# A graph and feed-forward kernel on one core: count chunks and checks moved ahead of the attention terms, and four PSUM banks for turned blocks

## The chip, the cores and the metric

The kernel runs on one core of a Trainium2 chip. The metric is the device time of one execution in microseconds (us), as the median of repeated runs. One more execution was taken with the hardware profiler; all views below are of that one.

## The reference

The program applies four layers to 3125 nodes of 256 features each, with a residual around every layer: a graph attention network, a mixture of experts shared by all nodes, a graph convolution network and a routed mixture of experts. The change is at the very beginning of the first layer, whose first part is:

```python
h = (x @ W).reshape(N, H, C)                      # 4 heads of 256
al_s = jnp.einsum('nhc,hc->nh', h, a_src)
al_d = jnp.einsum('nhc,hc->nh', h, a_dst)
e = jax.nn.leaky_relu(al_s[src] + al_d[dst], NEG_SLOPE)
m = jax.ops.segment_max(e, dst, num_segments=N)
ex = jnp.exp(e - m[dst])
denom = jax.ops.segment_sum(ex, dst, num_segments=N)
alpha = ex / denom[dst]
out = jax.ops.segment_sum(h[src] * alpha[:, :, None], dst, num_segments=N)
```

There are 100,000 edges, sorted by destination. `x` is layer-normalized before it enters. The same edges serve the second attention and the convolutions, so the kernel counts them once into a matrix.

## The kernel before, in words

Nodes are padded to 25 blocks of 128 rows. Edges are worked in 391 chunks of 256 (two tiles of 128). The class that the change touches runs two things at once in one long loop. The first is counting: for each chunk VectorE (and partly ScalarE) makes one-hot rows of the edges' keys, TensorE multiplies them into a PSUM bank, ScalarE copies most columns of the result into an accumulator in SBUF and VectorE adds the shared first column. `count_step(i)` (line 1738 on) is a software pipeline of that: it makes chunk i (lines 1669, 1672, for later chunks also 1675 and 1678 on ScalarE), multiplies chunk i-1 (1686), adds chunk i-3 (1708) and keeps chunk i-2 (1703). Hot rows have three buffers, the PSUM results three banks. Chunks below 20 take both one-hot parts from VectorE; of later ones two in three take the second part from ScalarE.

The second is the sum over edges for the attention: `edge_step` gathers the source rows with their attention terms by an indirect DMA on GpSimd (1797), weighs them, spreads the weights and multiplies (1863, 1869), and adds into sums per destination (1880). One edge step covers one chunk of the edges that do not belong to the first two blocks of destinations; those two blocks are done densely (2045), once the first piece of counts is finished.

Ahead of the loop lies a stage called `before` (the function `run`). In it x is loaded and normalized block by block and the edges' keys are made (`keys`, 1508 to 1525). The projections of x onto the attention vectors are needed for every node: `u1` holds W1 times the attention vectors (1573), each of the 25 blocks of x is turned by TensorE (2138), copied by ScalarE out of PSUM (2142), and multiplied by `u1` into one PSUM bank `pl` (2146). The turned blocks are also stored to DRAM in groups of five (2144). VectorE then copies `pl` to `sd` (2151), and `first_terms` reduces maxima (1587 to 1590), takes them over the partitions on GpSimd (1592), and makes the terms (1599 to 1614); the source terms go into the gathered table (1601), the destination terms and the weights of the nodes' loops into tables of their own (1605, 1615). Between its two halves six count steps run.

Two more things are in that stage: `edge_starts` with `check` (1465 to 1493), which work out on one partition where each chunk's edges begin and whether the shortcuts hold, and `attention_vectors("2", ...)`, which prepares W2's vectors for the second attention (line 1573 again, from W2 loaded at 2125).

After the stage, `open_sums` takes banks and buffers for the edge sums and clears two banks (1764), the first 24 tiles of rows are gathered, `new_sums(0)` begins the first sums with the loops of the first nodes (1912 to 1939, which wait for the loads 1921 and 1923), with one count step for each of its five tasks, and two more count steps follow. Then the loop runs one count step in each iteration. The edge steps are spread over it: 45 over the iterations from `i0` to `d1`, a fixed count, and the rest by the chunk's number.

What sets the order: on VectorE the stage `before` keeps the order in which it is written (`k.in_order` over that engine). On the other engines a scheduler places instructions when the program is built, by their dependences and the pools' buffers. Instructions of `open_sums` that need nothing from the stage may also be placed inside it. In the loop, TensorE, VectorE and ScalarE keep the written order. SyncE (SP) issues most DMAs, in one order of its own.

Of the kernel before, what the change touches and what calls it, by code (L numbers as in the profile page):

```python
# [19 lines left out]
PSUM = bass.MemoryType.PSUM  # L20
# [1373 lines left out]
class FirstLayer:  # L1394
# [698 lines left out]
    def run(self, src_cols, dst_cols, dst_rows, x_in, keep, stats, u2):  # L2093

        tc, nc, k, I = self.tc, self.nc, self.k, self.I
        with ExitStack() as ctx:
            pool = ctx.enter_context(tc.tile_pool(name="edges", bufs=1, reuse_waits="tile"))
            self.open_counts(ctx, pool)
            w1 = pool.tile([P, 2, 4 * D], F32, name="w1_all")
            with tc.tile_pool(name="before", bufs=1, reuse_waits="tile") as tmp, \  # L2100
                    tc.tile_pool(name="ps_in", bufs=1, space=PSUM, reuse_waits="tile") as psum, \
                    tc.tile_pool(name="ps_turn", bufs=2, space=PSUM, reuse_waits="tile") as turn:
                start = len(nc.cur_bb.bb.instructions)
                self.bounds(dst_rows, tmp)
                self.load_edges(src_cols, dst_cols, tmp)
                nc.gpsimd.dma_start(w1, I["L0_gnn_W1"].rearrange("(c p) f -> p c f", p=P))
                for b in range(0, NB, GB):
                    last_x = nc.sync.dma_start(
                        k.x[:, b:b + GB, :],
                        x_in[b * P:(b + GB) * P, :].rearrange("(b p) f -> p b f", p=P))  # L2110
                nc.vector.memset(k.rows[:, :, D:], 1.0)
                groups = [self.norm_rows(
                    k.x[:, b:b + GB, :],
                    self.table[b * P:(b + GB) * P, :D].rearrange("(b p) f -> p b f", p=P), tmp)
                    for b in range(0, NB, GB)]
                u1 = tmp.tile([P, 2, 8], F32, name="u1")
                for g in range(GR + 1):
                    if g < GR:
                        next(groups[g])
                    if g > 0:  # L2120
                        next(groups[g - 1])
                self.count_starts(tmp)
                self.attention_vectors("1", tmp, u1, w1.rearrange("p c (k f) -> p k c f", k=4))
                w2 = tmp.tile([P, 8, D], F32, name="w2")
                load = nc.gpsimd.dma_start(w2, I["L0_gnn_W2"].rearrange("(c p) f -> p c f", p=P))
                tc.add_manual_dep(load.ins, self.placed.ins.name, ORDER)
                tc.add_manual_dep(load.ins, last_x.ins.name, SYNC)
                self.keys(tmp)
                pl = psum.tile([P, 512], F32, name="pl")
                sd = tmp.tile([P, NB, 8], F32, name="sd")  # L2130
                i = 0
                for b in range(NB):
                    if b % 4 == 0:
                        self.count_step(i)
                        i += 1
                    pt = turn.tile([P, 512], F32, name="turn")
                    for c in range(2):
                        nc.tensor.transpose(pt[:, ts(c, P)], k.x[:, b, ts(c, P)], k.ident)
                    if b % GB == 0:
                        xt5 = tmp.tile([P, 2, GW], F32, name="xt", bufs=GR)  # L2140
                    xt = xt5[:, :, ts(b % GB, P)]
                    nc.scalar.copy(xt, pt[:, :2 * P].rearrange("p (c n) -> p c n", c=2))
                    if b % GB == GB - 1:
                        nc.sync.dma_start(self.turned[:, :, (b + 1) * P - GW:(b + 1) * P], xt5)
                    for c in range(2):
                        nc.tensor.matmul(pl[:, 8 * b:8 * b + 8], lhsT=xt[:, c, :],
                                         rhs=u1[:, c, :], start=(c == 0), stop=(c == 1))
                self.edge_starts(tmp)
                self.check(tmp)
                self.attention_vectors("2", tmp, u2, w2.rearrange("p (k c) f -> p k c f", c=2))  # L2150
                nc.vector.tensor_copy(sd.rearrange("p b k -> p (b k)"), pl[:, :8 * NB])
                parts = self.first_terms(sd, pool)
                next(parts)
                for _ in range(6):
                    self.count_step(i)
                    i += 1
                next(parts)
                k.in_order({}, start, [mybir.EngineType.DVE])
            self.open_sums(ctx, w1, stats)
            for c in range(RB * BC):  # L2160
                self.fetch(c)
            for task in self.new_sums(0):
                task()
                self.count_step(i)
                i += 1
            self.tasks.extend(self.new_sums(1))
            for m in range(2):
                for c in range(self.size[m]):
                    self.window(m, c)
            self.count_step(i)  # L2170
            i += 1
            self.place_edges(0)
            self.pick_terms(0)
            self.count_step(i)
            i += 1
            self.place_edges(1)
            self.weigh_edges(0)
            self.spread_edges(0)
            self.open_dense()
            e = s = 0  # L2180
            i0, d0 = i, CUT[1] + 6
            engines, last = [mybir.EngineType.PE, mybir.EngineType.DVE, mybir.EngineType.Activation], {}
            start = len(nc.cur_bb.bb.instructions)

            d1 = d0 + 3
            while i < C1 + 3 or e <= NE or s < len(self.steps) or self.tasks or self.later:
                if i < C1 + 3:
                    self.count_step(i)
                self.counted = i >= C1 + 3
                if i == d0:  # L2190
                    self.lead(0)
                later, self.later = self.later, []
                if self.tasks:
                    self.tasks.popleft()()
                share = (FIRST * (i - i0) / (d1 - i0) if i < d1 else
                         FIRST + (NE + 1 - FIRST) * (i - d1) / (C1 - d1))
                while e <= NE and e <= share:
                    self.edge_step(e)
                    if e == NE:
                        last_piece = self.through_w1(AS - 1)  # L2200
                        self.tasks.extendleft(reversed(last_piece[:-8]))
                        self.tasks.extend(last_piece[-8:])
                    e += 1
                while s < len(self.steps) and i > d0 + 3 and \
                        s * (C1 - 12 - d0) <= (i - d0 - 3) * len(self.steps):
                    self.dense_step(s)
                    s += 1
                for f in later:
                    f()
                start = k.in_order(last, start, engines)  # L2210
                i += 1
# [490 lines left out]
```

## Time and profile before

| | |
|---|---|
| median of 3 runs | 2530.82 us (2530.34 to 2532.02) |
| the profiled execution's own time | 2636.26 us |
| its span | 2634.5 us |
| mean granted TensorE clock in it | 0.931 |
| busy: TensorE, VectorE, ScalarE, GpSimd | 86%, 52%, 44%, 32% |

The profiled execution is 105 us longer than the median, so a sum made from its durations stands against 2636.26 first.

The stretches at the start, from the view of busy time by windows (us busy of each engine, granted clock, share of the DMA engines):

| stretch, us | PE | DVE | ACT | POOL | clock | DMA |
|---|---|---|---|---|---|---|
| 42.8 to 52.4 | 9.59 | 9.39 | 0.00 | 0.00 | 1.00 | 0.49 |
| 52.2 to 68.5 | 16.30 | 0.32 | 4.84 | 0.00 | 1.00 | 0.22 |
| 68.3 to 84.4 | 3.16 | 15.33 | 1.71 | 0.00 | 1.00 | 0.11 |
| 84.4 to 98 | 4.94 | 12.78 | 4.91 | 2.13 | 1.00 | 0.32 |
| 98 to 131 | 7.13 | 13.22 | 3.23 | 23.79 | 1.00 | 1.03 |

How to read the profile: a row of the timeline gives the start and the duration in us, the engine, the line in the kernel's source, the operation with its output and inputs, and how many were merged (x). What stands in brackets is how long the engine stood idle before, and which instruction, of which engine, released it. PE is TensorE, PEld its weight loads, DVE VectorE, ACT ScalarE, POOL GpSimd, SP SyncE; SPq rows are DMA issues. A transfer's own duration isn't in these rows.

### The profile page before, as it was taken

Reading aid. Unit: us, or ns where it says so; the run is one execution under the profiler, and the core shown is the slowest. Engines: PE = TensorE matmul, PEld = TensorE weight load, DVE = VectorE, ACT = ScalarE, POOL = GpSimd, SP = SyncE. Lnnn points to the kernel's source line nnn. Section 1 sums busy time; section 2 is a strip of 40 time slices with the busy share of each in tenths; the row PEclk is TensorE's granted clock in tenths of the full one; section 3 lists DMA queues with packets and bytes.
Section 4 is the critical chain, followed back from the end, with each engine's and each line's share of the span. In section 5 each row is a group of like instructions: output and inputs, shape, how many; then the busy total and the mean of one; then the engine's idle time right before and its main releaser. Section 6 shows DMA issues by size and latency. Waiting matters only on the chain. (4 is left out here: it accounts for less than half of the span.)

```text
span 2634.5 us, 38636 instructions
## 1 busy us (share of the span) xinstructions
PE 2263.8 (86%) x11821; PEld 1827.0 (69%) x11821; DVE 1376.1 (52%) x4332; ACT 1153.5 (44%) x2553; POOL 833.4 (32%) x805
## 2 busy tenths in 40 slices
PE   4277789888888888598999989979999998999997
PEld 4155566666666665387888768868877666888886
DVE  6666657466776786514888833433335654111110
ACT  3167655545555554342444434543433434222221
POOL 1465566666676775010000030000001122212221
PEclk9977988888989998899999989989999988999998
DMA  6633446464656665499221110004324426666662
GB/s 219 88 103 89 128 108 183 114 179 119 173 158 175 190 175 149 131 378 304 81 75 63 50 36 0 1 31 145 114 100 139 140 100 195 168 186 180 175 193 54
DMA packets 241723, 354.97 MB, mean 135 GB/s; under 512 B 45360, under 2 KB 182931, under 8 KB 237794
## 3 DMA queue, kind: packets, MB, share of 16 engines
q1 hardware_dynamic: 197762, 253.10, 30.6%
q0 software_dynamic: 40176, 94.81, 14.2%
q10 hardware_dynamic: 3568, 4.47, 0.7%
q8 instruction: 99, 1.62, 0.3%
q14 instruction: 118, 0.97, 0.1%
HBM read 266.60 MB, written 86.86 MB: 134 GB/s over the span
## 5 line engine op out<-in xcount | busy, mean ns | idle before, releaser
L1797 POOL DMA_INDIRECT edge_rows<-table,pick x566 | 608.7, 1075 | 320.2 <-PE edge_sums L1863 107.6
L1863 PE MATMUL edge_sums<-edge_moves,edge_rows 128*128 128x120 f32 x2264 | 351.6, 305 | 37.1 <-DVE agg L1880 30.6
L1863 PEld LDWEIGHTS edge_sums<-edge_moves,edge_rows 128*128 128x128 f32 x2264 | 327.2, 217 | 74.3 <-DVE agg L1880 41.6
L1092 PE MATMUL po<-parts,cnt_r 128*128 128x512 f32 x1250 | 328.2, 416 | 9.4 <-ACT cnt_r L1086 9.4
L1686 PE MATMUL ps<-hot_key,hot_lo 128*128 128x350 f16 (+2 forms) x782 | 205.3, 356 | 106.1 <-DVE acc L1708 49.2
L1703 ACT CAST acc<-ps 128x325 f32 (+2 forms) x391 | 178.1, 455 | 255.5 <-DVE acc L1708 111.9
L1092 PEld LDWEIGHTS po<-parts,cnt_r 128*128 128x128 f32 x1250 | 239.4, 197 | 70.6 <-ACT cnt_r L1086 10.2
L854 PE MATMUL po<-h,w 128*128 128x257 f32 x1250 | 277.5, 382 | 6.7 <-DVE w L845 4.4
L854 PEld LDWEIGHTS po<-h,w 128*128 128x128 f32 x1250 | 236.5, 191 | 43.1 <-DVE w L845 6.4
L1669 DVE TENSOR_SCALAR hot_key<-iota_key,key 128x350 f16<-128x350 f16 (+2 forms) x782 | 231.5, 324 | 34.1 <-PE ps L1686 25.6
L2578 ACT ACTIVATE hid<-ph,ffn_b 128x256 f32<-128x256 f32 x232 | 109.9, 474 | 298.2 <-PE ph L2576 298.2
L2576 PE MATMUL ph<-xe,ffn_w 128*128 128x256 f32 x928 | 210.1, 382 | 2.0 <-DVE xe L2555 2.0
L2586 PE MATMUL py<-ffn_w,hid 128*128 128x256 f32 x928 | 209.5, 384 | 0.0
L2590 POOL DMA_INDIRECT out<-y,to x58 | 90.4, 1558 | 350.1 <-DVE y L2589 269.1
L2576 PEld LDWEIGHTS ph<-xe,ffn_w 128*128 128x128 f32 x928 | 173.9, 191 | 28.9 <-DVE xe L2555 2.2
L2586 PEld LDWEIGHTS py<-ffn_w,hid 128*128 128x128 f32 x928 | 176.5, 193 | 23.4
L1686 PEld LDWEIGHTS <-hot_lo 128*128 128x128 f16 x782 | 62.4, 104 | 160.0 <-issue 60.4
L839 ACT ACTIVATE z<-z,att_cols 128x640 f32<-128x640 f32 x125 | 103.1, 828 | 153.0 <-DVE z L837 130.1
L1675 ACT ACTIVATE hot_lo<-iota_key,lo 128x128 f16<-128x128 f16 x494 | 169.0, 391 | 0.0
L1880 DVE TENSOR_TENSOR agg<-agg,edge_sums 128x126 f32 (+1 forms) x283 | 87.0, 307 | 145.4 <-PE edge_sums L1869 43.9
L1086 ACT CAST cnt_r<-cnt_h 128x1920 fp32r<-128x1920 f16 x50 | 89.9, 1799 | 133.4 <-PE po L1092 130.4
L2045 PE MATMUL po<-x_rows,w 128*128 128x257 f32 x400 | 129.5, 451 | 3.6 <-issue 3.6
(403 smaller groups left out, 3368.2 us busy)
## 6 DMA issues: line engine op xcount, KB each, us to landing
ffn_w<-in_L_ffn_W SPq DMA_DIRECT2D x58, 1024.0 KB
cnt_h<-cnt SPq DMA_DIRECT2D x50, 800.0 KB
rows<-blank SPq DMA_DIRECT2D x109, 258.0 KB
cnt<-acc SPq DMA_DIRECT2D x50, 400.0 KB
cnt<-cnt SPq DMA_DIRECT2D x25, 800.0 KB
normed<-first_out SPq DMA_DIRECT2D x20, 640.0 KB
first_out<-first SPq DMA_DIRECT2D x56, 192.0 KB
edge_rows<-table,pick POOLq DMA_INDIRECT x566
```

Source lines behind the costliest of these rows:

```text
L854: nc.tensor.matmul(pos[i][:, :D + 1], lhsT=w[:, ts(i, P)], rhs=moving[:, j, :D + 1], start=(j == 0), stop=(j == NB - 1))
L1092: nc.tensor.matmul(pos[b], lhsT=c[:, j - j0, ts(b, P)], rhs=parts[i][:, j].rearrange("p a m -> p (a m)"), start=(j == 0), stop=(j == NB - 1))
L1669: nc.vector.tensor_scalar(h[:, u, :NB * w], self.wide[:, :NB * w], self.key[:, t:t + 1], None, op0=ALU.is_equal)
L1675: nc.scalar.activation(l[:, u, :], self.wide[:, :P], AF.Abs, bias=self.lo[:, t:t + 1], scale=-1.0)
L1686: self.nc.tensor.matmul(ps[:, :n], lhsT=l[:, u, :], rhs=h[:, u, :n], start=(u == 0), stop=(u == CT - 1))
L1703: self.nc.scalar.copy(self.acc[g][:, :, ds(o + 1, width(c) - 1)], self.parts[c][:, :, 1:])
L1797: self.nc.gpsimd.indirect_dma_start(out=self.ring[:, e % (RB * BT), :], out_offset=None, in_=self.table, in_offset=bass.IndirectOffsetOnAx ...
L1863: nc.tensor.matmul(ps[:, f * 4 * w:f * 4 * w + EW], lhsT=self.rows_of(m)[:, e, ts(f, P)], rhs=self.spread[m % 2][:, e * 4 * w:e * 4 * w + EW],
L2045: self.nc.tensor.matmul(self.pos[i][:, :D + 1], lhsT=w[:, ts(i, P)], rhs=self.k.rows[:, j, :], start=(j == 0), stop=(j == NB - 1))
L2576: nc.tensor.matmul(ph, lhsT=w1[:, c, ts(f, P)], rhs=xe[:, c, :], start=(c == 0), stop=(c == 1))
L2578: nc.scalar.activation(hid[:, f, :], ph, AF.Gelu, bias=b1[:, f:f + 1])
L2586: nc.tensor.matmul(py, lhsT=hid[:, f, ts(i, P)], rhs=w2[:, f, :], start=(f == 0), stop=(f == NF - 1))
```

## The change

In the stage before the loop, the seven count steps that stood in the loop over the 25 blocks (one at every fourth block) become two, ahead of that loop. The edges' starts, the checks and W2's vectors, which stood behind the loop over blocks, come ahead of it, behind these two count steps. The six count steps between the halves of the terms stay where they are, and all later count steps follow on with the next chunk's number, so that the loop begins with chunk 15 instead of chunk 20. The pool of PSUM banks for turned blocks gets four banks instead of two. Lines behind the block loop have numbers lower by one after the change; those inside it are higher by two.

```diff
-                    tc.tile_pool(name="ps_turn", bufs=2, space=PSUM, reuse_waits="tile") as turn:
+                    tc.tile_pool(name="ps_turn", bufs=4, space=PSUM, reuse_waits="tile") as turn:
...
                 self.keys(tmp)
+                for i in range(2):
+                    self.count_step(i)
+                i = 2
+                self.edge_starts(tmp)
+                self.check(tmp)
+                self.attention_vectors("2", tmp, u2, w2.rearrange("p (k c) f -> p k c f", c=2))
                 pl = psum.tile([P, 512], F32, name="pl")
                 sd = tmp.tile([P, NB, 8], F32, name="sd")
-                i = 0
                 for b in range(NB):
-                    if b % 4 == 0:
-                        self.count_step(i)
-                        i += 1
                     pt = turn.tile([P, 512], F32, name="turn")
...
                         nc.tensor.matmul(pl[:, 8 * b:8 * b + 8], lhsT=xt[:, c, :],
                                          rhs=u1[:, c, :], start=(c == 0), stop=(c == 1))
-                self.edge_starts(tmp)
-                self.check(tmp)
-                self.attention_vectors("2", tmp, u2, w2.rearrange("p (k c) f -> p k c f", c=2))
                 nc.vector.tensor_copy(sd.rearrange("p b k -> p (b k)"), pl[:, :8 * NB])
```

## The prediction, made before the changed kernel ran

> **What bounds the kernel now.** The whole page comes first: 2634.5 us of span, PE 86% busy, DVE 52%. Its chain of waits names a stretch of the last DMA only, so it says nothing about the start. The change lies in the first 130 us, so I went to the timelines of that stretch, engine by engine. VectorE:
>
> ```profile
> 45.28 0.75 DVE L1515 TENSOR_TENSOR rel<-dst,key 128x566 f32<-128x566 int32 x1
> ...
> 50.37 0.27 DVE L1669 TENSOR_SCALAR hot_key<-iota_key,key 128x200 f16<-128x200 f16 x1
> ...
> 68.87 0.27 DVE L1669 TENSOR_SCALAR hot_key<-iota_key,key 128x200 f16<-128x200 f16 x1 [16.34 <-PE ps L1686]
> ...
> 72.05 0.29 DVE L1465 TENSOR_SCALAR begin<-ends_all 1x283 f32<-1x283 f32 x1
> ...
> 78.86 0.40 DVE L1573 SCALAR_TENSOR_TENSOR att_scr<-w,att 128x256 f32<-128x256 f32 x1
> ...
> 84.39 0.35 DVE L2151 COPY sd<-pl 128x200 f32<-128x200 f32 x1
> ```
>
> VectorE has made three chunks by 52.5 us, then stands 16.34 us until TensorE has multiplied chunk 0 (there are three buffers of hot rows). Behind this wait are queued four more chunks, the starts and checks (L1465 on), W2's vectors (L1573) and the copy of the attention sums (L2151). TensorE shows why it is late:
>
> ```profile
> 38.83 2.27 PE L2138 MATMUL turn<-ident,x_rows 128*128 128x128 f32 x8 [1.91 <-ACT xt L2142]
> 42.81 9.56 PE L2146 MATMUL pl<-u,xt 128*128 128x8 f32 x44 [1.71 <-DVE att_scr L1573]
> 52.23 0.67 PE L2138 MATMUL turn<-ident,x_rows 128*128 128x128 f32 x2
> ...
> 66.77 1.71 PE L2146 MATMUL pl<-u,xt 128*128 128x8 f32 x8
> 68.33 1.16 PE L1686 MATMUL ps<-hot_key,hot_lo 128*128 128x200 f16 x6
> ```
>
> With two banks twelve of 25 blocks are turned before the small products begin; thirteen follow, alternating with products. The chunks come behind all of it, at 68.3. SyncE's and GpSimd's timelines say who waits for 84.4:
>
> ```profile
> 92.72 0.37 SPq L1601 DMA_DIRECT2D table<-s_terms  x1
> ```
> ```profile
> 97.96 1.23 POOL L1797 DMA_INDIRECT edge_rows<-table,pick  x1 [2.96 <-PE ps L1686]
> ```
>
> The rows' terms are stored after the copy, and the first gather starts 5.2 us after that issue. So the copy at 84.39 sets the gathers, and they the loop.
>
> [...] checks that need nothing from chunk 0 ran only after the 16.34 us. [...] Three for counts, one for sums and two for turned blocks make 6; with four, 8. No bank is free then for the two edge sums that are cleared early (L1764). In the kernel before these memsets ran at 7.22 and 8.56 us, unwaited. [...] between 94 and 131 us engines are nearly always busy at 133 GB/s, with 9,645 of 12,457 packets under 512 B.
>
> **Part by part.** VectorE's order in the changed program is written out by its build: 2 chunks, starts, checks, vectors, copy, 6 chunks. I use the trace's durations.
>
> Removed ahead of the copy: 50.37 to 72.05 is 21.68 us for seven chunks with the stall. Two chunks take 50.37 to 51.75, 1.38. That is 20.30 saved, as long as no other wait takes its place.
>
> Unchanged work behind: starts and checks 72.05 to 78.86, 6.81; vectors 78.86 to 84.39, 5.53.
>
> Four banks: TensorE's order becomes nearly all transposes, then the products. Four blocks took 2.27 us, 0.57 each. With four banks two more blocks are turned before 38.83, so block 22 ends near 38.8 + 13 x 0.57 = 46.2, and block 24 near 47.4. With no lead it would be 1.1 later. Fifty products at 9.56/44 = 0.217 take 10.9: done at 58 to 60. The copy comes at about 66, so 6 to 8 us of VectorE's work covers this end; were that gone, the products would set it.
>
> New wait: L1764's first memset now stands right ahead of L1515 (45.28) and waits for ScalarE's copy of block 22. That copy took 0.37: 46.6 to 47.7, a stall of 1.3 to 2.4; never below nothing, since VectorE is there at 45.3. I take 1.5. All keys, chunks, checks and the sums' copy are queued behind. The two memsets, 0.23 each, were in an idle stretch and now add 0.4. Sum for the copy: 20.3 - 1.5 - 0.4 = 18.4 us earlier, at 66.0.
>
> Moved transfers: W2's own load on GpSimd's queue keeps its place (issued at 25.90), and its vectors ask for it at about 60.5 instead of 78.86. DMA was idle by 47.5 in the trace, so it had landed. Three stores of turned blocks on SyncE, 640 KB each, move from 52 to 68 into 43 to 48 us; at the 340 GB/s of that stretch they add 5.8 us of traffic, so W2 lands at worst near 53.5. Seven us of cover; cost nothing.
>
> Behind the copy: reductions, six chunks and terms ran 84.39 to 92.72, 8.3 us, with one add fewer now; I leave it equal. GpSimd's part, with its 7.00 us gap before L1774 (ready at 94.9 for a gather at 97.96), shifts along. What is late next is the gathers and their terms' transfers, a DMA stretch that starts 18.4 us earlier.
>
> SyncE's order there changes: the loops' weights (L1615), before issued at 94.84, now stand behind two loop_x (128 KB each) and two edge_turn loads (32 KB each). VectorE waits for them: L1933 at 115.21 after 13.50 of idling for by_node. 320 KB at 340 GB/s are 0.9; four issues of about 0.35 to 0.55 are 1.8. They move ahead, they aren't added, so 0 is the low end. At the high end SyncE's loop_x pair, which took 96.73 to 104.45, holds them for its 7.7. I take 1.0.
>
> Given back: thirteen chunks stood ahead of the stage that opens the sums, now eight. Five move into the main loop; seven lie in the stage between in both. The order after the first piece of counts is the same. From 150 to 270 us ScalarE kept 90 chunks (L1703):
>
> ```profile
> L1703 ACT CAST acc<-ps 128x175 f32 (+1 forms) x90 | 31.1, 345 | 26.7 <-DVE acc L1708 9.8 <-PE ps L1686 8.8 <-PE edge_sums L1863 2.7
> ```
>
> That is 120/90 = 1.33 us each, with a share of 35 edge steps in it, and these number the same after. So 1.33 is the high end, 6.7 for five. VectorE's own part is 0.69 of making and 0.11 of adding, 0.8 or 4.0. Were the loop held by gathers, they would be free: zero. I take 1.0 each, 5.0 in all.
>
> Sum: 18.4 - 1.0 - 5.0 = 12.4 us. The profiled execution would go from 2636.26 (2634.5 of span and 1.8 around it) to 2623.9. The median is 2530.82, 105 lower; the stretch concerned has a granted clock of 1.00 and is mostly VectorE, ScalarE and DMA, so I carry 12.4 over unscaled: **2518.4 us**.
>
> **The rivals.**
> - All of the front's gain is kept: the five chunks fill waits that the loop has anyway. GpSimd waits 31.8 us for edge sums between 140 and 270, and every engine idles a fourth or more there; against it, those waits are for TensorE itself, which also multiplies chunks. 18.4 alone: 2512.4.
> - The new DMA order takes the gain: loops' weights wait the 7.7 us behind loop_x, chunks cost 1.33, the memset 2.4: 20.3 - 2.8 - 7.7 - 6.7 = 3.1, so 2527.7, no change. For it speak the full DMA engines there; against it, that what stands ahead is small and the queue has the same bytes in either order.
> - Slower: TensorE's granted clock. It is 1.00 to 130 us and 0.67 to 0.83 from 140 to 260. If idling ahead of the loop is what buys the later clock, 18 us less of it lower the mean of 0.931. If the whole span went with the clock, 12.4 us are 0.0044 of it: from 0.9266 down the change loses. At 0.923 it is 2634.5 x (0.931/0.923 - 1) = 22.8, less 12.4: 2541.2. Against it, the clock returns to 1.00 at 260 to 280 us while TensorE is still 71% busy.
> - That the change doesn't do what it says: VectorE's order is fixed and shows the move, so this has no chance of its own.
>
> **The numbers.** About 0.2% (5.1 us) is what a measurement of this kernel can tell from no change. Forecast 0.71 (2511 to 2525), all kept 0.12, DMA order 0.10 (2526 to 2533), clock 0.07. Faster is the first two, 0.83; same 0.10; slower 0.07. The range 2509 to 2527 leaves out the last and most of the third, some 0.16, and a little below.
>
> **What would show it.** In the profile after: no 16 us wait at L1669; a wait of 1.3 to 2.4 us at the first L1764; the sums' copy at 65 to 67.5; products done before 61; the first gather at 79 to 81; L1933 first at 96 to 99; the first dense products (before at 302.5) 11 to 14 us earlier, and every later stage by as much. I'd be wrong if W2's vectors wait for DMA, if L1933 isn't earlier by 15 us, if the loop's chunks take over 2 us each, or if the mean clock moves by more than 0.004.

## The result, and the profile after

The changed kernel takes 2513.10 us (median of 6 runs) against 2530.58 us (median of 6) for the kernel before beside it: ratio 0.9935, 95% interval 0.9915 to 0.9954, so 16.4 us faster (11.6 to 21.5); the two medians lie 17.5 us apart. Two more comparisons, told of below, gave 0.9927 (0.9905 to 0.9950) and 0.9919 (0.9900 to 0.9938). The prediction was 2518.4 with a range from 2509 to 2527: right in direction, 4 to 5 us short in size. The profiled execution took 2512.02 us, its span is 2510.2 us, its mean granted clock 0.930.

First a thing about the two profiles. The one shown ahead of the change (2636.26 us) fits a second level of times, which a later run showed: on one chip (number 5) the same kernel takes 2638 us, with all runs between 2629 and 2655, while on three others (0, 3 and 14) it takes 2531. The chip of that first profile is not on record. Up to the first gather both levels show the same times, to 0.2 us, so those lines can be compared; later ones can't. For those I use a profile of the kernel before taken at the 2531 level (the run "before, third" below).

VectorE's timeline of the changed kernel, over the lines shown of the kernel before:

```profile
45.10 0.23 DVE L1764 MEMSET edge_sums<- 128x200 f32 x1
45.24 0.73 DVE L1515 TENSOR_TENSOR rel<-dst,key 128x566 f32<-128x566 int32 x1
46.01 0.23 DVE L1764 MEMSET edge_sums<- 128x200 f32 x1
...
50.42 0.27 DVE L1669 TENSOR_SCALAR hot_key<-iota_key,key 128x200 f16<-128x200 f16 x1
...
51.80 0.29 DVE L1465 TENSOR_SCALAR begin<-ends_all 1x283 f32<-1x283 f32 x1
...
58.61 0.40 DVE L1573 SCALAR_TENSOR_TENSOR att_scr<-w,att 128x256 f32<-128x256 f32 x1
...
64.14 0.35 DVE L2150 COPY sd<-pl 128x200 f32<-128x200 f32 x1
...
93.59 1.97 DVE L1933 TENSOR_TENSOR agg<-loop_x,by_node 128x1024 f32<-128x1024 f32 x1 [13.03 <-DMA by_node<-loops]
```

No row up to the copy has a bracket: VectorE doesn't stand between 45 and 64 us. The 16.34 us wait for chunk 0 is gone, nothing took its place, and the sums' copy starts at 64.14 instead of 84.39. TensorE's timeline shows why VectorE finds them ready:

```profile
38.65 5.17 PE L2140 MATMUL turn<-ident,x_rows 128*128 128x128 f32 x27 [1.91 <-ACT xt L2144]
...
44.16 15.99 PE L2148 MATMUL pl<-u,xt 128*128 128x8 f32 x98
60.00 0.83 PE L1686 MATMUL ps<-hot_key,hot_lo 128*128 128x200 f16 x4
```

The turning is interrupted only once, by two products; then nearly all small products come in one piece, and they end at 60.15, 4 us ahead of the copy. ScalarE's timeline has the turned blocks' copies in one piece as well:

```profile
38.24 6.57 ACT L2144 COPY xt<-turn 128x256 f32<-128x256 f32 x19
```

They end by 44.81, before VectorE asks for the banks at 45.10: hence no wait at L1764. SyncE's queue and GpSimd's show what follows from the copy:

```profile
71.89 0.36 SPq L1601 DMA_DIRECT2D table<-s_terms  x1
```
```profile
77.15 1.20 POOL L1797 DMA_INDIRECT edge_rows<-table,pick  x1 [2.39 <-PE ps L1686]
78.66 0.97 POOL L1797 DMA_INDIRECT edge_rows<-table,pick  x1 [0.30 <-issue]
```

The terms are stored 20.83 us earlier (92.72 before), and the first gather is 20.81 us earlier (97.96 before). That is the gain of the front. On VectorE, apart from the two memsets, only the number of chunks ahead of the copy has changed: starts, checks and W2's vectors stand between chunks and copy in both timelines. Two chunks fit into the three buffers of hot rows, so nothing waits for TensorE. The question is what becomes of the gain.

### The profile page after: what moved, and what is told of

It is laid out like the page before. It is cut to its first block, busy times and chain, and to the rows that moved or that the text cites. A ratio compares the mean times of both kernels' runs of the same rounds, so it can differ in the third digit from the quotient of the medians.

```text
span 2510.2 us, 38638 instructions
## 1 busy us (share of the span) xinstructions
PE 2215.2 (88%) x11821; PEld 1797.8 (72%) x11821; DVE 1375.5 (55%) x4332; ACT 1150.1 (46%) x2553; POOL 830.2 (33%) x805
## 5 line engine op out<-in xcount | busy, mean ns | idle before, releaser
L1863 PE MATMUL edge_sums<-edge_moves,edge_rows 128*128 128x120 f32 x2264 | 333.9, 295 | 18.1 <-DVE agg L1880 17.9
L1863 PEld LDWEIGHTS edge_sums<-edge_moves,edge_rows 128*128 128x128 f32 x2264 | 313.6, 208 | 47.6 <-DVE agg L1880 25.4
L1686 PE MATMUL ps<-hot_key,hot_lo 128*128 128x350 f16 (+2 forms) x782 | 198.2, 345 | 65.8 <-ACT hot_lo L1678 35.7
L2585 PEld LDWEIGHTS py<-ffn_w,hid 128*128 128x128 f32 x928 | 176.3, 193 | 23.3
L1086 ACT CAST cnt_r<-cnt_h 128x1920 fp32r<-128x1920 f16 x50 | 89.8, 1799 | 130.3 <-PE po L1092 121.2
L1686 PEld LDWEIGHTS <-hot_lo 128*128 128x128 f16 x782 | 60.8, 103 | 115.7 <-ACT hot_lo L1678 51.0
L1708 DVE TENSOR_TENSOR acc<-acc,ps 128x25 f32 x391 | 101.2, 259 | 48.8 <-ACT acc L1703 45.8
```

The source lines that it names most:

```text
L1686: self.nc.tensor.matmul(ps[:, :n], lhsT=l[:, u, :], rhs=h[:, u, :n], start=(u == 0), stop=(u == CT - 1))
L1863: nc.tensor.matmul(ps[:, f * 4 * w:f * 4 * w + EW], lhsT=self.rows_of(m)[:, e, ts(f, P)], rhs=self.spread[m % 2][:, e * 4 * w:e * 4 * w + EW],
L2585: nc.tensor.matmul(py, lhsT=hid[:, f, ts(i, P)], rhs=w2[:, f, :], start=(f == 0), stop=(f == NF - 1))
```

## Where the 20.8 us go

The same two kernels on one chip (number 14; the runs "before, third" and "after, third"). VectorE's and TensorE's timelines of the kernel before:

```profile
84.37 0.35 DVE L2151 COPY sd<-pl 128x200 f32<-128x200 f32 x1
...
114.76 1.98 DVE L1933 TENSOR_TENSOR agg<-loop_x,by_node 128x1024 f32<-128x1024 f32 x1 [13.37 <-DMA by_node<-loops]
...
977.06 0.26 DVE L1708 TENSOR_TENSOR acc<-acc,ps 128x25 f32 x1 [0.72 <-ACT acc L1703]
```
```profile
286.89 1.14 PE L2045 MATMUL po<-x_rows,w 128*128 128x257 f32 x4 [1.99 <-DVE w L2036]
```

and of the changed one:

```profile
64.47 0.35 DVE L2150 COPY sd<-pl 128x200 f32<-128x200 f32 x1
...
94.19 1.98 DVE L1933 TENSOR_TENSOR agg<-loop_x,by_node 128x1024 f32<-128x1024 f32 x1 [13.31 <-DMA by_node<-loops]
...
961.56 0.26 DVE L1708 TENSOR_TENSOR acc<-acc,ps 128x25 f32 x1 [0.72 <-ACT acc L1703]
```
```profile
270.46 2.08 PE L2045 MATMUL po<-x_rows,w 128*128 128x257 f32 x4 [1.99 <-DVE w L2036]
```

The rows are marks along the program: the sums' copy, the first nodes' loops (L1933), the first dense product (L2045), the last chunk's add (L1708). The changed kernel has three profiles at the 2531 level (the first one, "after, again" and "after, third", on more than one chip), which tell how far one profile can be trusted; the kernel before has one:

| mark | before, third | after: first, again, third | mean of after, less before |
|---|---|---|---|
| sums' copy | 84.37 | 64.14, 64.12, 64.47 | -20.1 |
| first gather | 97.93 | 77.15, 77.12, 77.44 | -20.7 |
| L1933 first | 114.76 | 93.59, 93.71, 94.19 | -20.9 |
| first dense product | 286.89 | 268.65, 270.22, 270.46 | -17.1 |
| last chunk added | 977.06 | 957.73, 958.44, 961.56 | -17.8 |
| span | 2528.2 | 2510.2, 2509.6, 2516.0 | -16.3 |

Up to L1933 everything is kept. Between L1933 and the first dense product 3.8 us are given back; after that nothing is lost or won beyond the three profiles' own scatter (2 us at the dense products, 4 at the last chunk, 6 at the end). Counted from the first edge sums' product (L1863), it is 5.1: this product comes at 104.00, 104.11 and 104.60 instead of 126.41, so 22.2 us earlier.

## The experiments

The theory: VectorE's time ahead of the sums' copy sets the gathers, and the only thing paid for it is the five chunks that the loop now has to count. Rivals: the loop hides the chunks (all is kept); the DMA order takes the gain; the clock does.

**Before, again** (the kernel before, unchanged): was the 2636 us profile an odd execution?

> The kernel before, once more, for a second profiled execution: the first one took 2636.3 us, 105 over the median of its timed runs, and the changed kernel's profiled execution took 2512.0, at its median. Theory (front): the 105 us belong to that one execution, so a second profile lies at 2516 to 2540 us, with the sums' copy again at 84 to 85 us and the first dense product at 290 to 300. Rival (loop): the changed program makes the whole loop faster, and a second profile of before lies above 2600 again. Ratio to before 1.000, within 0.003.

Measured: 2638.18 us, ratio 1.0001 (0.9983 to 1.0019); span 2637.6, copy at 84.24, first gather 97.81, L1933 114.64, first dense product 303.41, last chunk 1080.51. The timed runs beside it have a median of 2637.93. So the second profile lies above 2600, as the rival said, but not for its reason: the kernel before is just as long in its timed runs. The three runs after this one were on that chip too (number 5), in the same hour; whether the level belongs to the chip or to its state then can't be told. All others, on the chips 0, 3 and 14, stand beside a kernel before of 2531.

**Two banks**: the changed kernel with the banks put back.

```diff
-  tc.tile_pool(name="ps_turn", bufs=4, ...
+  tc.tile_pool(name="ps_turn", bufs=2, ...
```

> The changed kernel with two banks for turned blocks instead of four. Theory: TensorE's order is the old one (24 transposes, then in turns with products), so the products end near 68.3 us as before, VectorE reaches the copy at 63.7 (no memsets among the keys) and waits about 4.7 for TensorE: copy at 68.4 instead of 64.1, and the whole some 4.2 us slower than the changed kernel: ratio to before 0.9951. Rival (banks are nothing): same as the changed kernel, 0.9935. Rival (banks are most of it): the wait of 16 us only moves to the copy, ratio above 0.998.

Measured: 2624.91 us, ratio 0.9944 (0.9929 to 0.9959). VectorE's timeline, and the end of the products in TensorE's:

```profile
68.13 0.37 DVE L2150 COPY sd<-pl 128x200 f32<-128x200 f32 x1 [4.35 <-PE pl L2148]
```
```profile
66.38 1.71 PE L2148 MATMUL pl<-u,xt 128*128 128x8 f32 x8
```

With two banks turning and products alternate as before and end at 68.1; VectorE is at the copy 4.35 us earlier and waits. So the order alone brings 16.1 us at the copy (84.24 to 68.13), and the banks move the products' end from 68.1 to 60.15, out of the copy's way: 4 us. This is read at the copy; the changed kernel itself didn't run on this chip, and in the times 0.9944 can't be told from its 0.9919 to 0.9935. Fewer chunks without the other moves weren't tried.

**Banks only**: the kernel before with four banks.

```diff
-  tc.tile_pool(name="ps_turn", bufs=2, ...
+  tc.tile_pool(name="ps_turn", bufs=4, ...
```

> The kernel before with four banks for turned blocks and nothing else. Theory: VectorE still waits for chunk 0 behind TensorE's products, but these end at 60 to 62 instead of 68.3, so the copy comes 6 to 8 us earlier than 84.4 and nothing is given back later: ratio to before 0.997. Rival (the wait goes with the banks): the copy comes 15 us earlier or more, 0.994. Rival (the early memsets, now waiting for the banks, eat it): 1.000.

Measured: 2637.48 us, ratio 0.9994 (0.9981 to 1.0007). VectorE's timeline, then TensorE's:

```profile
62.95 0.23 DVE L1764 MEMSET edge_sums<- 128x200 f32 x1 [15.29 <-ACT xt L2142]
...
83.81 0.35 DVE L2151 COPY sd<-pl 128x200 f32<-128x200 f32 x1
```
```profile
44.09 13.23 PE L2146 MATMUL pl<-u,xt 128*128 128x8 f32 x62
...
65.31 2.57 PE L2146 MATMUL pl<-u,xt 128*128 128x8 f32 x12
67.73 1.16 PE L1686 MATMUL ps<-hot_key,hot_lo 128*128 128x200 f16 x6
```

This is the wait that I had feared for the changed kernel, in full size: the early memset of a sum's bank stands 15.29 us for ScalarE's copy of a turned block; no bank was free for it sooner, because most of the blocks are turned only after 62 small products. With two banks for turned blocks the two memsets ran at 7.22 and 8.56 us without a wait. This wait takes the place of the one for chunk 0, and the copy is 0.4 us earlier. Alone, four banks are worth nothing, as the second rival said; the products don't end earlier either (67.9).

**Five in the gap**: the changed kernel with five more chunks, meant for the place where VectorE waits 13 us for the first loads of the loops' weights; the loop then begins with chunk 20, as in the kernel before.

```diff
-            for task in self.new_sums(0):
+            for n, task in enumerate(self.new_sums(0)):
                 task()
-                self.count_step(i)
-                i += 1
+                for _ in range(6 if n == 0 else 1):
+                    self.count_step(i)
+                    i += 1
```

> The changed kernel with the five chunks that it gave to the loop put into the stretch where VectorE idles 13.0 us for the loops' rows, ahead of the loop; the loop starts with chunk 20 again. Theory: they cost 0.8 us of VectorE each there, 4.0 of the 13, and are hidden, and the loop is five steps shorter: 5 us faster than the changed kernel (3 to 6.7), ratio to before 0.9915. Rival (the chunks were free in the loop): no faster than the changed kernel, 0.9935. Rival (TensorE or ScalarE is held up ahead of the edge sums): slower than it, above 0.995.

Measured: 2615.69 us, ratio 0.9908 (0.9881 to 0.9934); copy 64.02, first gather 77.02, L1933 at 93.94 after 13.15 us of waiting. The wait is as long as without the five, and the trace says why: they aren't in it. VectorE has made 15 chunks ahead of L1933, as in the changed kernel, and makes the five behind its start. VectorE's timeline of the same kernel at the 2531 level ("five again"):

```profile
80.30 0.45 DVE L1672 TENSOR_SCALAR hot_lo<-iota_key,lo 128x128 f16<-128x128 f16 x1
94.29 1.98 DVE L1933 TENSOR_TENSOR agg<-loop_x,by_node 128x1024 f32<-128x1024 f32 x1 [13.54 <-DMA by_node<-loops]
...
98.33 0.26 DVE L1669 TENSOR_SCALAR hot_key<-iota_key,key 128x200 f16<-128x200 f16 x1
```

The stretch from L1933 to the first edge sums' product (L1863) grows from 10.4 to 12.7 us, by 0.46 for each chunk. What the five save in the loop lies behind that, so this run doesn't show that the wait hides chunks.

**After, again**: the changed kernel, unchanged, beside the next three.

> The changed kernel, unchanged, on the chip of the runs around it. If the gain is a property of the program: ratio to before 0.9935 (0.9925 to 0.9945), copy of the sums (L2150) at 64.0 to 64.3, first gather at 77.0 to 77.3, L1933 at 93.5 to 94.1, whatever the level of the chip. If the level of the chip matters to the gain, because the time after the first 130 us is stretched by some other amount: ratio outside 0.992 to 0.996, with the same starts up to 94 us.

Measured: 2512.20 us, ratio 0.9927 (0.9905 to 0.9950); copy 64.12, gather 77.12, L1933 93.71.

**Vectors late**: W2's vectors go behind the attention terms. (The recorded text says behind the maxima; in the trace they stand from 70.07 to 75.6 us, behind the last term.)

```diff
-                self.attention_vectors("2", tmp, u2, ...)
                 pl = psum.tile([P, 512], F32, name="pl")
...
                 next(parts)
+                self.attention_vectors("2", tmp, u2, ...)
                 k.in_order({}, start, [mybir.EngineType.DVE])
```

> W2's vectors are made behind the maxima, while GpSimd takes these over the partitions. Theory (the copy's start sets the gathers, whatever stands ahead of it on VectorE): the copy moves from 64.1 to 60.2, where the products (end near 60.0) set it and no longer VectorE, with a wait on PE of about 1.5 us; first gather at 73.2, L1933 at 90; ratio to before 0.9920, 4 us less than the changed kernel. Rival (the gap behind the maxima is already filled by six chunks, so 5.5 us of vectors there make the terms late): the store of the source terms stays at 71.9, the first gather at 77, ratio 0.9935. Second rival (the saving is hidden behind the loads for L1933): gather at 73 but L1933 at 93.6.

Measured: 2514.41 us, ratio 0.9941 (0.9923 to 0.9958). VectorE's and GpSimd's timelines:

```profile
60.29 0.37 DVE L2149 COPY sd<-pl 128x200 f32<-128x200 f32 x1 [1.65 <-PE pl L2147]
```
```profile
73.32 3.48 POOL L1797 DMA_INDIRECT edge_rows<-table,pick  x1 [1.70 <-issue]
77.10 0.95 POOL L1797 DMA_INDIRECT edge_rows<-table,pick  x1 [0.30 <-issue]
```

The copy is where the theory put it, set by the products now, and the first gather is issued at 73.3. But this gather takes 3.48 us where the changed kernel's takes 1.20, so the second starts at 77.10 against 78.66: of 3.8 us 1.6 are left. What makes it so long isn't shown. L1933 is at 89.71, 4.1 earlier, but the first edge sums' product at 103.08 is only 1.0 earlier (104.11 in "after, again"), and the first dense product, at 268.56, is inside the changed kernel's own scatter. So the theory holds up to L1933, and the saving is lost behind it, where neither rival looked. No gain can be measured.

**Both**: vectors late and five in the gap together.

> W2's vectors behind the maxima, and five more chunks in the wait for the loads of the first sums. If both act and add: 4 us from the first and 5.0 us (five at 1.0) from the second below the changed kernel, ratio to before 0.9900. If a chunk in the loop costs only 0.5 us: 0.9910. If the vectors' move is worth nothing: the ratio of the five chunks alone, 0.9908 as measured before.

Measured: 2504.26 us, ratio 0.9899 (0.9883 to 0.9915); L1933 at 88.31, first dense product 261.81, last chunk 949.41.

**Ten in the gap**: as five in the gap, with `range(11 if n == 0 else 1)`.

> Ten more chunks than the changed kernel has in the wait for the loads of the first sums (the loop begins with chunk 25). VectorE needs 0.7 us for each, 7 us in a wait of 13 us, so they should still be hidden: L1933 at 93.6 to 94.2. If a chunk in the loop costs 1.0 us: 10 us below the changed kernel, ratio 0.9896, 5 us below the five. If it costs 0.5: 0.9916. Rival (the loop is held by gathers and edge steps, not by chunks): no more than the changed kernel, 0.9935; the five's 0.9908 was then scatter. Second rival (hot rows and banks fill up, so VectorE waits and L1933 comes later): L1933 later than 95.

Measured: 2506.50 us, ratio 0.9892 (0.9876 to 0.9908); L1933 at 96.47, first dense product 265.04, last chunk 951.19. VectorE has made 19 chunks ahead of L1933, so four of the ten are in the wait, which is 11.52 us here. This profile's whole start is 0.7 us late (copy 64.94); L1933 comes 1.9 us later than that explains. The second rival's sign (later than 95) came, but VectorE isn't what makes L1933 late: it still waits for by_node, whose load was issued 1.0 us later behind the copy than in the changed kernel. Why isn't shown.

**Before, third; after, third; five again**: the three on one chip.

> The kernel before, unchanged, beside the changed one and the five chunks on one chip, for profiles that can be set against each other. Ratio 1.000. If the chip is the quick one (2531 us timed before): the last piece of counts ends near 975, 17 us behind the changed kernel's 958; if it is the other (2638), near 1080, as before. In both the starts up to the first gather are as known: copy 84.2 to 84.4, gather 97.8 to 98.

> The changed kernel, unchanged. Ratio 0.9931 (0.992 to 0.9945). Against the kernel before on this chip its last count (L1708) should end 20.8 us (first gather) less five chunks at 1.0 to 1.4, so 13.8 to 15.8 us earlier, and nearly all of the gain in the time should be there at that point. If the gain or a loss arises after the counts, theory of the front is incomplete.

> The changed kernel with five more chunks in the wait for the loads, so that the loop begins with chunk 20 like the kernel before: beside the changed kernel on one chip it gives the price of five chunks in the loop directly. At 1.0 each: ratio to before 0.9911 and 5 us below the changed kernel; at 1.33 (the upper bound from ScalarE's pace): 0.9905; at zero: 0.9931. Against the kernel before it has the same count of chunks ahead of the loop, so its gain is the front's alone: 20.8 us, 0.9918, if that is kept whole.

Measured: 2529.68 us, ratio 0.9995 (0.9982 to 1.0009); 2513.51 us, 0.9919 (0.9900 to 0.9938); 2511.68 us, 0.9927 (0.9908 to 0.9945). By the times five chunks more or less can't be told apart here: 0.9908 and 0.9927 with them, 0.9935, 0.9927 and 0.9919 without. The traces can tell more. The time to the first dense product, at the 2531 level, from two marks:

| kernel | loop begins with chunk | from L1933, us | from L1863, us |
|---|---|---|---|
| after (three profiles) | 15 | 175.1, 176.5, 176.3: mean 176.0 | 164.7, 166.1, 165.9: mean 165.5 |
| five again | 20 | 266.56 - 94.29 = 172.3 | 159.6 |
| before, third | 20 | 286.89 - 114.76 = 172.1 | 160.5 |
| ten in the gap | 25 | 265.04 - 96.47 = 168.6 | 155.9 |
| vectors late | 15 | 268.56 - 89.71 = 178.9 | 165.5 |
| both (two profiles) | 20 | 261.81 - 88.31 = 173.5, 263.62 - 89.67 = 174.0 | 158.6, 159.2 |

From L1933 it falls by 3.7 for the first five and by 3.7 for the next: 0.74 us a chunk, what is left after the chunks' price at their new place. (For the next five it is less, 0.5, if counted from the copy, since ten move L1933 itself.) The kernel before, with the same chunk at the loop's start as five again, has the same length to 0.2. With late vectors it is 4.9 to 5.4, 1.0 to 1.1 each. From L1863, behind the moved chunks, a chunk is worth 0.7 to 1.4 us, and 1.0 between before and after. Most of these are single profiles, and the changed kernel's three differ by 1.5 us. At the 2638 level the stretch from L1933 doesn't depend on the chunks: 188.8 before, 188.6 with two banks (chunk 15), 188.9 with five in the gap (chunk 20). There, the rival that the loop hides them holds up to this mark.

**Both, again**: the version that looked best, once more.

> W2's vectors behind the maxima and five more chunks in the wait for the loads, a second time, since the vectors alone gave 0.9941 and both gave 0.9899. If both parts act (4 us from the vectors, 3.6 to 5 from the chunks, below the changed kernel's 0.9927): 0.9893 to 0.9897, and the first dense products at about 261, 8 us ahead of the changed kernel's 268 to 270. If the vectors' 4 us are lost again on the way and 0.9899 was scatter: 0.9910 to 0.9920, with the first dense products at 265 or later.

Measured: 2505.08 us, ratio 0.9903 (0.9878 to 0.9929); first dense product 263.62, last chunk 946.53. The middle of what was expected: earlier than five again by 2.9 us at the dense product, later than the 261 that all of both parts would give. Against the kernel before, two comparisons give 0.9899 and 0.9903. Its medians lie 7 to 9 us below those of the changed kernel; the intervals of the ratios touch, so this is likely, not shown, in times. The traces agree with it: 9.8 and 12.7 us earlier at the last chunk than the changed kernel's mean of 959.2.

## Why the prediction was right, and which terms were off

**The removed wait (20.30 us): right.** From the first chunk's start to the copy VectorE takes 13.72 us (64.14 - 50.42) instead of 34.02 (84.39 - 50.37). Two banks show the order to be the cause, banks only that the banks are not.

**The memset's wait (1.5): 0; the memsets (0.4): 0.24.** The wait's mechanism is real (15.29 us in banks only), its size here was wrong. I took the old pace of turning, 2.27 us for four blocks, and put ScalarE's copy of block 22 at 46.6. But the 27 transposes took 5.17, 0.38 a block, and 19 copies followed at 0.35 each, done at 44.81. The two memsets lengthen the stretch from L1514 to the first chunk from 5.42 to 5.66. Between the two profiles this doesn't show at the first chunk (50.42 against 50.37), since the later one has L1514 0.19 earlier.

**Products done at 58 to 60: hit, by two errors that cancelled, so by luck.** The timeline's 44, twelve times 4 and 8 records make 100, not fifty. A hundred at the 0.217 that I used are 21.7 us: they would have ended at 65.9 and held up the copy. They took 15.99/98 = 0.163 each, a mean of two paces: about half went at 0.112 each, twice the old pace, the others at 0.213. The recorded clock is 1.00 at the first and 0.50 at the second (last section); the prediction didn't have that. So the 6 to 8 us of cover were 4, and vectors late used them up.

**W2's load: no cost, right.** No row at L1573 waits. **Behind the copy, unchanged: right within 0.6**: copy to gather 13.0 against 13.6.

**Loops' weights behind other loads (1.0): 0.** L1933 is 20.9 earlier where the gather is 20.7 earlier, and it waits 13.31 against 13.37. SyncE's order did change: the weights' store (L1615) came 5.7 us behind that of the terms, not 2.1. But the loads (L1923), which wait for this store to land (4.4 us of SyncE's waiting), were issued at 89.8 to 90.3, as far behind the gather as before. So the rival that the DMA order takes the gain falls up to this mark.

**Five chunks given back (5.0): 3.8 from L1933, 5.1 from L1863**, so 0.76 or 1.0 each against the 1.0 chosen between 0.80 and 1.33. Right in kind; the size depends on the mark.

Together: 17.4 at L1933 was 20.9, 5.0 behind it was 3.8, so 12.4 was 17.1. The size was off mostly by the memset's wait and the loops' weights, 2.5 us that I put on the path and that cost nothing there, and by the 0.6 behind the copy. So copy, gather, L1933 and dense products all came earlier than the windows I gave for them. The time alone would have misled: 2513.1 is nearer to the rival that keeps all of the front (2512.4) than to my 2518.4, and only the trace shows that a larger gain was made and a part given back.

**The clock rival fell, and its premise was misread.** At the 2531 level the mean granted clock in the views went from 0.945 before to 0.930 (0.930, 0.927 and 0.930), more than the 0.004 that I called decisive, and the kernel got faster. Busy time by windows, before, third (columns: window, its length, each engine's busy time and instructions, clock, DMA share, GB/s):

```profile
44.00:60.00 16.00, 16.00 (x80) 16.00 (x80) 8.36 (x24) 2.26 (x7) 0.00 (x0) 1.00 0.34 125
60.00:95.00 35.00, 14.78 (x70) 11.22 (x70) 25.31 (x131) 7.96 (x20) 2.10 (x5) 1.00 0.13 40
95.00:150.00 55.00, 22.61 (x132) 15.26 (x133) 33.98 (x123) 18.04 (x60) 39.74 (x33) 1.00 0.83 138
...
300.00:950.00 650.00, 586.06 (x3995) 452.50 (x3994) 485.10 (x1626) 395.40 (x1038) 495.11 (x467) 0.94 0.62 175
```

and after, third:

```profile
44.00:60.00 16.00, 16.00 (x97) 16.00 (x96) 15.61 (x53) 0.70 (x3) 0.00 (x0) 0.64 0.38 149
60.00:95.00 35.00, 8.66 (x35) 3.54 (x35) 21.01 (x118) 6.29 (x17) 14.28 (x18) 0.50 0.72 77
95.00:150.00 55.00, 36.06 (x247) 27.28 (x247) 45.48 (x183) 30.42 (x102) 40.98 (x36) 0.71 0.50 139
...
300.00:950.00 650.00, 583.66 (x3969) 450.02 (x3968) 486.30 (x1617) 394.29 (x1032) 482.09 (x455) 0.94 0.62 174
```

The drop lies between 44 and 150 us: 16 x 0.36 + 35 x 0.50 + 55 x 0.29 = 39 us of clock, which is 0.0155 of 2516, all of it. But this is a difference of the records, not of the clock. The trace of before, third holds no clock record ahead of 142.2 us, that of after, third none ahead of 41.7, and the view counts a stretch without a record as 1.00. The 1.00 up to 130 us, which the prediction and the table of stretches have, is of that kind. The last section shows from durations that TensorE ran there at the pace of 0.50 (0.213 us from one small product to the next, as at a recorded 0.50), where its work can be compared. Counted as 0.50 up to each first record, the means would be 0.917 before and 0.922 after (an estimate from these records), so no drop. From 300 to 950 us, where the records are complete, the clock is 0.94 in both. That idling ahead of the loop buys clock later, on which this rival rested, was an assumption; no run shows it.

**What stays open.** Why the price of a chunk from L1933 shows at one level and not at the other; why VectorE makes the five chunks behind L1933; and whether the vectors' 1 to 4 us are worth having by themselves.

## What to carry to other kernels

On an engine that worked in order in the trace, as VectorE did here (the checks, which need nothing from chunk 0, ran only behind its 16.34 us), look for the wait behind which things are queued that don't need it, and put ahead of the critical result only what this result needs. What is pushed out has a price at its new place, so look for a wait there that hides it, and then look in the trace whether the work is where the edit meant it to be: of the ten chunks meant for VectorE's 13 us of idling, four stood in it, of the five none. And when one edit frees a buffer count and another an order, try each alone: here the banks alone gave nothing, the order alone 16 us at the copy, and only with the order did the banks give their 4.

## What the runs showed of the hardware that I had not expected

**One chip 4% behind three others.** The same kernel takes 2638 us on chip 5 and 2531 on chips 0, 3 and 14, at mean clocks in the views of 0.929 and 0.945. Up to the first gather the profiles agree to 0.2 us; of 109 us between the spans (2637.6 and 2528.2) 103 are there when the last chunk is added (1080.51 and 977.06). Between 300 and 950 us the clock is 0.90 on chip 5 and 0.94 in before, third. What TensorE waited for from 300 to 900 us on chip 5, from the view of its waits (total, times, longest):

```profile
...
PE ps L1686 <- issue: 9.1, 5, 4.9
PE aux L1831 <- issue: 7.8, 9, 4.2
PE edge_sums L1863 <- issue: 7.3, 10, 1.3
...
PE aux L2065 <- issue: 5.4, 2, 3.0
```

"Issue" is time in which the engine waited for nothing that the profile shows. These four rows are 29.6 us of it; the same view of before, third has 0.7. It is part of the difference; what makes it wasn't found. For the reader: first see on which chip a profile was taken.

**A clock of 1.00 that was no record.** The kernels whose turning runs on (after, five, ten, late, both) show 0.50 from about 50 to 95 us; those that alternate show 1.00. The durations tell which to believe. The small products in the changed kernel, from the view of busy time for their line (window, its length, TensorE's busy time and records, those of its weight loads, clock, DMA share, GB/s):

```profile
46.00:48.00 2.00, 2.00 (x21) 2.00 (x20) 1.00 1.04 405
...
52.00:54.00 2.00, 2.00 (x11) 2.00 (x11) 0.50 0.00 0
```

and in before, third:

```profile
46.00:48.00 2.00, 2.00 (x11) 2.00 (x11) 1.00 0.78 300
```

In the changed kernel the number of products halves when the recorded clock does: from start to start they take 0.112 us at 1.00 and 0.213 at 0.50 (medians). In the kernel before they take 0.213 at a "1.00" without a record. The edge sums' products say the same. The changed kernel has two groups of eight, one at a recorded 0.50, one at 1.00:

```profile
104.00 2.04 PE L1863 MATMUL edge_sums<-edge_moves,edge_rows 128*128 128x120 f32 x8
...
109.64 1.05 PE L1863 MATMUL edge_sums<-edge_moves,edge_rows 128*128 128x120 f32 x8
```

and before, third has its first without a record:

```profile
126.41 2.04 PE L1863 MATMUL edge_sums<-edge_moves,edge_rows 128*128 128x120 f32 x8
```

The changed kernel's record has 0.50 in one piece from 49.6 to 107.6 us. The durations agree with it, as far as TensorE works in it; what misled was the stretch ahead of the first record.

**Small products at which TensorE reads fully busy, and the clock falls.** In the changed kernel the record begins with 1.00 at 42.7 us, after 4 us of turning without a break, and goes to 0.50 at 49.6, in the middle of the small products, though TensorE isn't idle before 60.8. In the other two profiles of this kernel the stretch of 1.00 is 41.9 to 48.7 and 41.7 to 48.6. In banks only, 62 such products in one piece take 13.23 us, 0.213 each, and no record begins before 144.7 us. So the banks' 4 us at the copy go together with a faster TensorE for 7 us; how much is owed to that and how much to the order wasn't separated.
